# Attention and feed-forward sandwich: the last rows in a new order, the very last by column halves, x loaded by halves, w_o by one part a block

## The chip, the cores and the metric

The kernel runs on one core of one Trainium2 chip. The metric is the device time of one execution in microseconds (us), as a median over several runs. The engines of the core go by the profile's short names: PE (TensorE, matmuls and transposes through a matmul), PEld (its weight loads, which overlap PE), DVE (VectorE), ACT (ScalarE), POOL (GpSimd) and SP (SyncE, which here only issues DMAs).

## What is computed

One transformer layer over x, 1024 rows of 512 columns, all in fp32. The reference, shortened:

```python
x = x + layernorm(attention(layernorm(x), w_q, w_k, w_v, w_o))
x = x + layernorm(ffn(x, base_W, base_b, router_W, router_b, A, B, expert_map))

def attention(h, w_q, w_k, w_v, w_o):      # 32 query heads, 8 key/value heads of 128
    q, k, v = h @ w_q, h @ w_k, h @ w_v    # 4 query heads share one k, v
    scores = where(causal, q @ k.T / sqrt(128), -inf)
    return softmax(scores) @ v @ w_o

def ffn(x, ...):
    base_out = x @ base_W.T + base_b
    p = softmax(x @ router_W.T + router_b)       # 15 logits
    w = per-expert sums over expert_map of the 8 largest p   # 8 experts
    lora = ((x @ A.T) * w) @ B * 2               # rank 16 for each expert
    return base_out + lora
```

## The kernel before

**Tiling.** The 1024 rows are NT = 8 row tiles of 128. A key/value head with its R = 4 query heads is a group; there are G = 8. A block (g, t) is one group and one row tile; the list `blocks` has N = 64 of them, group by group. The first six groups take the row tiles in order. The last two (from block N2 on) go together by pairs of row tiles, in the order 0, 3, 2, 1, so that the row tiles of the last eight blocks can be finished one after the other. The last four rows to finish are c, d, e and f, row tiles 4, 5, 2 and 3, which belong to blocks N-6, N-5, N-2 and N-1.

**One block.** A block's scores are made in four sub-blocks (32 rows of each of the four heads): scores `s` on PE, the causal mask (L618) and the negated maximum `nmax` (L620) on DVE, the exponentials `p` with their sum on ACT (L625), the reciprocal `rec` (L631) on DVE, the product with it on ACT (L632), and a transpose within 32 x 32 squares into `T` (L638) on DVE. Where a sub-block doesn't reach the end of its row tile, POOL clears the rest of `p` (a memset, L623). Sixteen small DMAs, nearly all on SP, then bring `T` to the tile `K` with keys on partitions (`K<-T`). Two blocks later PE multiplies by `v` into `po`, ACT copies that to `attnT` (L669), and the output projection follows: for two row tiles at once in `project_o_pair`, which needs four sums and differences of `attnT` (L720 to L723, on DVE: sums, sums, attnT, sums) and has the products `pa` to `pe`, each added into `acc` by DVE (L744), for the last group by itself in `project_o` (`pO`). Projections of later blocks fill in on PE. Products of halves save matmuls: combined weights and inputs are made on POOL (`tx` by L188; `sq` and others by `combine_q`, L145; `combine_o`, L706).

**Order.** Every engine carries out its instructions in order. In the main loop the order comes from the loop itself and from a scheduler that sorts the instructions of each engine, save those given to `keep`, which stay in the order of the code. `loads(i)` issues the weight loads of later blocks at the head of block i, on SP. Loads of w_o: `load_o(g)` issues R = 4 parts of 256 KB (128 partitions of 512 fp32); it is called for g + 1 in the row t = 5 of the groups 0 to 5.

**Start.** x comes in by eight row-tile loads, alternately on SP and on ACT's queue, with the first weights between them. After a layer norm each row tile is transposed by PE (`ptx_x`); PE fills the time before with 26 transposes of the identity, `idle`.

**Last rows.** After the loop the order on all engines is written out: `run(pieces)` emits the pieces of PE work with what belongs to them; `go(rows)` emits the next deferred piece of a row's DVE, ACT and POOL work (`held`), and `work_off` emits deferred pieces within the scores. The pieces of a row after its attention: `ffn_norms` (statistics L288, normalising L300, adding x L777), `ffn_router` (transposes `ptx_h`; `pl`, the router's logits with the experts' first products; `route`, L813 to L830, softmax and the eight largest, which ends in `hw`), and `ffn_out` (`base`, the four pairs of `pf`; `turn_hw`, transpose `ptw` and copy `hwT`, L857; `finish`, the last pair of `pf` with `bt_sb`, the addition of the bias to `y`, L864, and the layer norm). For rows c, d, e that norm's scaling is on ACT (L303, L304) and its addition to `acc` on POOL (L870); for row f both are on DVE (L300, L870). The power -1/2 of every norm (`rstd`, L294) is on POOL. `ffn_store` stores a finished row. L103, L106 and L109 are the helpers of all matmuls, transposes and DMAs.

PSUM banks: `bank` gives the next of a ring of single banks in turn, so a product can start when the one that had that bank is read out; `ps_s` is the pool of the scores, whose tiles serve some `pf` as well.

Of the kernel before, what the change touches and what calls it, by code (L numbers as in the profile page):

```python
# [22 lines left out]
def kernel(  # L23
# [175 lines left out]
        for c in range(KC // 2):  # L199
            weights["v", gv, i * (KC // 2) + c] = w[:, c, :]  # L200

    def load_o(g, by=nc.scalar):
        wo = wp.tile([P, R, H], F32, tag="wo", name=f"wo_{g}")
        for j in range(R):
            load(wo[:, j, :], w_o[ts(g * R + j, P), :], by)
        weights["o", g] = wo

    def load_base(tag, cs, by=nc.scalar):
        for c in cs:
# [4 lines left out]
    x_in = turn_tile("K", "x", NT - 1).rearrange("p (t h) -> p t h", t=NT)  # L214
    two = (nc.sync, nc.scalar)

    def load_x(t):
        load(x_in[:, t, :], x[ts(t, P), :], two[t % 2])

    for t in range(2):  # L220
        load_x(t)
    for i in range(2):
        load_v(0, i, two[i])
    for t in range(2, TPB):
        load_x(t)
    load_k(0, nc.sync)
    for i in range(2):
        load_q(0, i, two[1 - i])
    for t in range(TPB, NT):
        load_x(t)  # L230

    ident = const.tile([P, P], F32, tag="ident", name="ident")
    make_identity(nc, ident)
    neg_half = const.tile([P, 1], F32, tag="neg_half", name="neg_half")
    nc.gpsimd.memset(neg_half, -0.5)

    xnT = [big.tile([P, KC, QB], F32, tag=f"xnT{b}", name=f"xnT_{b}") for b in range(NQB)]

# [362 lines left out]
    def scores(g, t, j):  # L601

        n = t * P + (j + 1) * SQ
        full = (t + 1) * P
        name = f"{g}_{t}_{j}"
        s = ps_s.tile([P, S], F32, tag="s", name=f"s_{name}")
        for c0 in range(0, n, QB):
            w = min(QB, n - c0)
            matmul(
                s[:, c0 : c0 + w],  # L610
                qTs[g, t // 2][:, (t % 2) * NSUB + j, :, :].rearrange("p h q -> p (h q)"),
                kTs[g, c0 // QB][:, :w],
                start=True,
                stop=True,
            )
        pin = keep if blocks.index((g, t)) >= N2 + 2 else lambda ins: ins
        rescale_scores()
        keep(nc.vector.tensor_tensor(s[:, n - SQ : n], s[:, n - SQ : n], smask, ALU.add))  # L618
        nmax = small.tile([P, 1], F32, tag="nmax", name=f"nmax_{name}")
        keep(nc.vector.tensor_reduce(nmax, s[:, :n], AX.X, ALU.max, negate=True))  # L620
        p = act.tile([P, S], F32, tag="p", name=f"p_{name}", bufs=3)
        if n < full:
            nc.gpsimd.memset(p[:, n:full], 0.0)  # L623
        total = small.tile([P, 1], F32, tag="total", name=f"total_{name}")
        keep(nc.scalar.activation(p[:, :n], s[:, :n], AF.Exp, bias=nmax, accum_out=total))  # L625
        finish_scores()
        work_off(1 + len(deferred) // 5)

        def rescale():
            rec = small.tile([P, 1], F32, tag="rec", name=f"rec_{name}")  # L630
            keep(nc.vector.reciprocal(rec, total))  # L631
            keep(nc.scalar.mul(p[:, :n], p[:, :n], rec))  # L632

        def finish():
            if j == 0:
                turned[g, t] = turn_view(turn_tile("T", g, t), t)
            pin(
                nc.vector.transpose(  # L638
                    turned[g, t][:, :, j, :, :].rearrange("p b k q -> p k b q"),
                    p[:, :full].rearrange("p (k b q) -> p k b q", b=R, q=SQ),  # L640
                )
            )
            if j == NSUB - 1:
                three = (nc.sync, nc.sync, nc.gpsimd)

                at = blocks.index((g, t))
                short = at < 1 or at < N2 and g % 2 and t in (1, 2, 3)
                alone = not short and at < N - 1
                to_keys(g, t, by=three[:1] if alone else three)

        score_tile["rescale"], score_tile["finish"] = rescale, finish
# [59 lines left out]
    def project_o_pair(g, u):  # L711

        hk = R // 2
        wo, wt = weights["o", g], weights["ot", g]
        a1 = attnT.pop((g, 2 * u)).rearrange("p (h q) -> p h q", q=P)
        a2 = attnT.pop((g, 2 * u + 1)).rearrange("p (h q) -> p h q", q=P)
        a11, a12, a21, a22 = a1[:, :hk], a1[:, hk:], a2[:, :hk], a2[:, hk:]
        sums = act.tile([P, 3, hk, P], F32, tag="sums", name=f"sums_{g}_{u}", bufs=1)
        s1, s2, s4 = (sums[:, n] for n in range(3))
        nc.vector.tensor_tensor(s1, a21, a22, ALU.add)  # L720
        nc.vector.tensor_tensor(s2, s1, a11, ALU.subtract)
        nc.vector.tensor_tensor(a21, a11, a21, ALU.subtract)
        nc.vector.tensor_tensor(s4, a12, s2, ALU.subtract)  # L723
        b11, t12, b21, b22 = wo[:, :hk, :hn], wo[:, :hk, hn:], wo[:, hk:, :hn], wo[:, hk:, hn:]
        to = sums_o[u]
        pm = {}

        def product(name, half, lhs, rhs, dst=None):


            def piece(k):
                if half == 0 and k == 0:
                    pm[name] = bank(f"p{name}_{g}_{u}").rearrange("p (a n) -> p a n", n=hn)
                matmul(
                    pm[name][:, half, :], lhs[:, k, :], rhs[:, k, :], start=(k == 0), stop=(k == hk - 1)
                )
                if k == hk - 1 and dst is not None:
                    src = pm[name][:, : half + 1, :]
                    if half == 0:
                        src = src.to_broadcast([P, dst.shape[1], hn])  # L740
                    if g == 0 and name in "ab":
                        nc.vector.tensor_copy(dst, src)
                    else:
                        nc.vector.tensor_tensor(dst, src, dst, ALU.add)  # L744

            return [(hn, lambda k=k: piece(k)) for k in range(hk)]

        def last():
            if g == G - 2:
                every = to[:, 0:1, :].to_broadcast([P, 4, hn])  # L750
                nc.vector.tensor_tensor(to[:, 1:, :], to[:, 1:, :], every, ALU.add)

        return (
            product("a", 0, a11, b11)
            + product("a", 1, a12, b21, to[:, 0:2, :])
            + product("b", 0, s2, wt[:, 1], to[:, 2:5, :])
            + product("c", 0, a21, wt[:, 0], to[:, 3:5, :])
            + product("d", 0, s1, t12, to[:, 2:5:2, :])
            + product("e", 0, s4, b22)
            + product("e", 1, a22, wt[:, 2], to[:, 2:4, :])  # L760
            + [(1, last)]
        )
# [77 lines left out]
    def ffn_out(t):  # L840
# [3 lines left out]
        def base(k):  # L844
            if k == 0:

                if t in (c, e, f):
                    pf.append(ps_s.tile([P, S], F32, tag="s", name=f"pf_{t}")[:, :512])
                else:
                    pf.append(bank(f"pf_{t}"))  # L850
            matmul(pf[0], state["hT", t][:, k, :], weights["base", k], start=(k == 0), stop=False)
# [9 lines left out]
        def finish():  # L861
            matmul(pf[0], state.pop(("hwT", t)), bt_sb, start=False, stop=True)
            y = ffn.tile([P, H], F32, tag="hy", name=f"y_{t}", bufs=3)
            order(nc.vector.tensor_tensor(y, pf[0], bias_bc, ALU.add))  # L864
            by = nc.vector if t == f else nc.gpsimd
            statistics, norm = layernorm(y, y, f"y{t}", nc.vector if t == f else nc.scalar)

            def add_y():
                norm()
                order(by.tensor_tensor(acc[t], y, acc[t], ALU.add))  # L870
                state["done", t] = True

            defer(t, statistics, add_y)

        w = [(512, lambda k=k: base(k)) for k in range(KC)]
        return w[:2], [(P, turn_hw)], w[2:], [(512, finish)]

    def ffn_store(t):
        assert state["done", t]
# [41 lines left out]
    def loads(i):  # L921
# [7 lines left out]
        if i < N2:  # L929
# [10 lines left out]
            if t == 6 and (g + 1) % GV == 0:  # L940
                for j in range(2):
                    load_v((g + 1) // GV, j, by)
            if t == 5:
                load_o(g + 1, by)
        elif i == N2 + 3:
            load_o(G - 1, by)
        elif i == N2 + 4:
            load_base("wk", (0, 1), by)
        elif i == N2 + 7:
            load_base("wv", (2, 3), by)  # L950
# [44 lines left out]
    run(first_q[: 2 * KC] + project_k(0, 0) + first_q[2 * KC :])  # L995
    for t in range(TPB, TPB + 2):
        input_turn(t)
    load_o(0, nc.sync)

    def complete(i, *behind):  # L1000

# [73 lines left out]
        ffn_store(t)  # L1075
    (turn_d, products_d), (turn_e, products_e), (turn_f, products_f) = map(ffn_router, (d, e, f))
    out_c, out_d, out_e, out_f = map(ffn_out, (c, d, e, f))
    run(o_pair[:8] + out_c[0] + out_c[2] + o_pair[8:16] + [turn_d] + o_pair[16:])
    run(attend(N - 2) + [products_d])
    go(d)  # L1080
    run(out_c[1] + project_o(*blocks[N - 2]))
    go(e)
    run(out_c[3])
    go(e, e)
    run(attend(N - 1) + project_o(*blocks[N - 1]))
    go(e, f, c, f, f)
    run(out_d[0] + out_d[1] + out_d[2] + [turn_e] + out_d[3])
    go(f, c)
# [1 line left out]
    go(d, e)  # L1090
    run(out_e[0] + out_e[2][:1] + [turn_f] + out_e[2][1:] + [products_f])
    go(d, f)
    run(out_f[0] + out_e[1] + out_f[2][:1] + out_e[3])
    go(e)
    run(out_f[2][1:] + out_f[1])
    go(e)
    run(out_f[3])
    go(f, f)
    for t in (c, d, e, f):
        ffn_store(t)  # L1100

# [40 lines left out]
```

## Time and profile before

| what | us |
|---|---|
| median of 3 runs | 1066.59 (1066.48 to 1067.16) |
| the profiled execution's own time | 1066.64 |
| its span, first to last instruction | 1064.9 |
| PE busy in the span | 1046.5 |
| end of the last matmul, from the span's start | 1055.74 |

The profiled execution is 0.05 us from the median. All times inside a trace are counted from the span's start; the execution's own time is 1.74 us more than the span. The granted TensorE clock was 0.996 of full speed. The costliest groups of the page's part 5 give the durations that recur below: after the line, the engine and the operation come the tiles written and read with their shapes, the count, then the busy time and the mean of one in ns, then the engine's idle time just before these instructions and what ended most of it:

```profile
L103 PE MATMUL po<-K,v 128*128 128x512 f32 x576 | 280.3, 594 | 1.7 <-DMA wo<-in_w_o_dram 1.0
L103 PE MATMUL s<-kT,qT 128*128 128x512 f32 (+15 forms) x768 | 272.4, 463 | 1.4 <-ACT p L625 1.3
L638 DVE STREAM_TRANSPOSE T<-p 128x128 f32<-128x128 f32 (+7 forms) x256 | 197.7, 774 | 52.5 <-ACT p L632 37.9
L188 POOL TENSOR_TENSOR tx<-xnT 128x256 f32<-128x256 f32 x52 | 37.9, 729 | 209.8 <-PE pv L103 124.6
```

A matmul's duration counts its pipeline too, so neighbours overlap: eight in a row of `pO` take 3.44 us and not eight times 0.6. What PE waited for, the ends of the critical stretches and the instructions that the change moves are shown in the prediction.

### The profile page before, as it was taken

The page shows a single profiled execution, that of the slowest core. Times are in us where ns is not written, and L with a number is a line of the kernel's source. Part 1 is how long each engine was busy: PE and PEld are TensorE (multiplying, and loading weights), DVE is VectorE, ACT ScalarE, POOL GpSimd, SP SyncE. Part 2 cuts the span into 40 slices and gives each one's busy share as a digit, 9 for nine tenths or more (in the row PEclk, how much of TensorE's full clock was granted, in tenths as well). Part 3 has the DMA queues.
Part 4 walks back from the last instruction along what each step waited for, and adds up shares of the span by engine and source line. Part 5 has one row for each costly group of instructions (what it writes and reads, how often), then busy time and mean ns, then how long its engine had stood idle before and what let it go on. Part 6 is the DMA issues. An engine that isn't in the chain of part 4 may idle for free.

```text
span 1064.9 us, 15423 instructions
## 1 busy us (share of the span) xinstructions
PE 1046.5 (98%) x4782; PEld 729.8 (69%) x4782; DVE 740.1 (70%) x1810; ACT 480.7 (45%) x965; POOL 255.0 (24%) x491
## 2 busy tenths in 40 slices
PE   9999999999999999999999999999999999999996
PEld 7766667767777676767777667767787566466553
DVE  4586657876687766877577776887457766576756
ACT  3655435553344534553245544554235554353421
POOL 2613125241131215241130313351130110111212
PEclk9999999999999999999999999999999999999998
DMA  5146352563125442463225352464523754444231
GB/s 188 34 115 149 70 121 70 150 154 86 27 56 154 104 108 72 115 158 79 61 50 131 102 125 61 127 160 109 129 66 104 183 143 111 125 110 106 69 84 40
DMA packets 78513, 111.99 MB, mean 105 GB/s; under 512 B 18176, under 2 KB 49920, under 8 KB 78432
## 3 DMA queue, kind: packets, MB, share of 16 engines
q1 hardware_dynamic: 74960, 105.71, 39.5%
q0 software_dynamic: 2096, 3.46, 1.4%
q10 hardware_dynamic: 1376, 1.84, 0.5%
q8 instruction: 39, 0.64, 0.3%
q14 instruction: 42, 0.34, 0.1%
HBM read 33.34 MB, written 2.10 MB: 33 GB/s over the span
## 4 chain that ended last, share of the span: by engine, by line
PE 90%; DVE 3%; SPq 3%; ACT 1%; DMA 1%; issue 1%; POOL 0%; POOLq 0%; DVEq 0%; ACTq 0%
PE po L103 22%; PE s L103 20%; PE pq L103 19%; PE pv L103 5%; PE pe L103 4%; PE pa L103 4%; PE pk L103 4%; PE pf L103 3%; PE pO L103 3%; SPq L109 3%; PE pc L103 2%; PE pb L103 2%; PE pd L103 2%; PE pl L103 1%; DMA wo<-in_w_o_dram 1%
## 5 line engine op out<-in xcount | busy, mean ns | idle before, releaser
L632 ACT ACTIVATE p<-p,rec 128x32 f32<-128x32 f32 (+31 forms) x256 | 188.3, 736 | 225.8 <-DVE rec L631 164.8
L103 PE MATMUL po<-K,v 128*128 128x512 f32 x576 | 280.3, 594 | 1.7 <-DMA wo<-in_w_o_dram 1.0
L103 PE MATMUL s<-kT,qT 128*128 128x512 f32 (+15 forms) x768 | 272.4, 463 | 1.4 <-ACT p L625 1.3
L625 ACT ACTIVATE p<-s,nmax 128x32 f32<-128x32 f32 (+31 forms) x256 | 179.5, 701 | 163.1 <-DVE nmax L620 147.2
L638 DVE STREAM_TRANSPOSE T<-p 128x128 f32<-128x128 f32 (+7 forms) x256 | 197.7, 774 | 52.5 <-ACT p L632 37.9
L103 PEld LDWEIGHTS s<-kT,qT 128*128 128x128 f32 x768 | 141.2, 190 | 118.2 <-issue 105.9
L620 DVE TENSOR_REDUCE nmax<-s 128x1 f32<-128x32 f32 (+31 forms) x256 | 180.2, 704 | 7.3
L103 PEld LDWEIGHTS po<-K,v 128*128 128x128 f32 x576 | 103.6, 190 | 61.7 <-issue 51.4
L623 POOL MEMSET p<- 128x96 f32 (+2 forms) x192 | 29.3, 157 | 423.2 <-DVE T L638 377.5
L618 DVE TENSOR_TENSOR s<-s,smask 128x32 f32<-128x32 f32 x256 | 48.0, 187 | 99.4 <-PE s L103 98.8
L103 PE MATMUL pq<-xnT,wq 128*128 128x128 f32 (+1 forms) x656 | 113.3, 321 | 0.0
L103 PEld LDWEIGHTS pq<-xnT,wq 128*128 128x128 f32 x656 | 99.5, 191 | 14.0 <-issue 7.2
L188 POOL TENSOR_TENSOR tx<-xnT 128x256 f32<-128x256 f32 x52 | 37.9, 729 | 209.8 <-PE pv L103 124.6
L450 DVE TENSOR_TENSOR qT<-pq,qT 128x256 f32<-128x256 f32 x138 | 62.0, 460 | 32.0 <-ACT qT L476 18.9
L669 ACT COPY attnT<-po 128x512 f32<-128x512 f32 x64 | 37.4, 584 | 76.5 <-PE po L103 76.3
L103 PE MATMUL pa<-wo,attnT 128*128 128x256 f32 x224 | 58.8, 385 | 0.0
L103 PEld LDWEIGHTS pq<-tx,wq 128*128 128x128 f32 x368 | 47.1, 192 | 7.6 <-issue 7.5
L103 PEld LDWEIGHTS pq<-tx,sq 128*128 128x128 f32 x368 | 47.5, 192 | 5.7 <-issue 5.0
L103 PE MATMUL pq<-tx,sq 128*128 128x128 f32 x368 | 51.2, 275 | 0.0
L103 PEld LDWEIGHTS pa<-wo,attnT 128*128 128x128 f32 x224 | 41.0, 190 | 14.0 <-issue 9.3
L625 ACT ACTIVATION_READ_ACCUMULATOR p<-s,nmax 128x1 f32 x256 | 49.5, 193 | 0.0
L103 PE MATMUL pq<-tx,wq 128*128 128x128 f32 x368 | 49.2, 275 | 0.0
(146 smaller groups left out, 1258.4 us busy)
## 6 DMA issues: line engine op xcount, KB each, us to landing
K<-T SPq DMA_DIRECT2D x128, 128.0 KB, 2.4
K<-T SPq DMA_DIRECT2D x128, 112.0 KB, 2.3
wq<-in_w_q_dram SPq DMA_DIRECT2D x27, 512.0 KB, 4.8
K<-T SPq DMA_DIRECT2D x128, 96.0 KB, 2.2
K<-T SPq DMA_DIRECT2D x128, 80.0 KB, 2.1
wo<-in_w_o_dram SPq DMA_DIRECT2D x32, 256.0 KB, 3.9
K<-T SPq DMA_DIRECT2D x108, 64.0 KB, 2.0
K<-T SPq DMA_DIRECT2D x113, 48.0 KB, 2.0
```

What stands on the lines that cost most here:

```text
L103: keep(nc.tensor.matmul(*args, **kw))
L109: keep(by.dma_start(dst, src))
L188: nc.gpsimd.tensor_tensor(dst, p, q, ALU.subtract)
L450: nc.vector.tensor_tensor(dst, src, to, ALU.add)
L618: keep(nc.vector.tensor_tensor(s[:, n - SQ : n], s[:, n - SQ : n], smask, ALU.add))
L620: keep(nc.vector.tensor_reduce(nmax, s[:, :n], AX.X, ALU.max, negate=True))
L623: nc.gpsimd.memset(p[:, n:full], 0.0)
L625: keep(nc.scalar.activation(p[:, :n], s[:, :n], AF.Exp, bias=nmax, accum_out=total))
L632: keep(nc.scalar.mul(p[:, :n], p[:, :n], rec))
L638: nc.vector.transpose(turned[g, t][:, :, j, :, :].rearrange("p b k q -> p k b q"), p[:, :full].rearrange("p (k b q) -> p k b q", b=R, q=SQ),)
L669: copy = nc.scalar.copy(o, po)
```

## The change

- **Start.** Row tiles 0 and 1 of x are loaded in two halves of 64 partitions each, one on SP, one on ACT's queue. Row tiles 4 to 7 all go to SP. ACT makes a copy of one column (`warm`) ahead of its other work.
- **w_o.** `load_o` takes the parts that it is to load: for groups 1 to 6 one part in each of the rows t = 4, 5, 6, 7. Group 0 and group 7 are loaded at once as before.
- **Last rows.** `work_off` is left out of the very last sub-block of scores. The four sums of the last pair are pinned in their place on DVE. Row c's four `pf` pairs follow `pa` (after four pieces instead of eight), row d's transposes follow the next six. `attend(N - 1)`, the `po` of the last block, stands ahead of the `finish` of row c.
- **Row f.** `ffn_out_last` makes `pf` in two halves of 256 columns in two banks. The bias and the statistics go by halves as well, all on DVE; then the mean is subtracted by a tensor_scalar, and a scalar_tensor_tensor multiplies by `rstd` and adds `acc` in one instruction, where a norm (tensor_scalar with mean and `rstd`) and an addition were. All of it is pinned.

In the scheduled order of instructions, PE and DVE have the same order as before between the start and the last rows. SP differs by the places of the w_o parts. POOL differs in the blocks (2, 6) and (4, 6), where `combine_q` stands ahead of a memset of `p` that it followed before.

```diff
-    def load_o(g, by=nc.scalar):
-        wo = wp.tile([P, R, H], F32, tag="wo", name=f"wo_{g}")
-        for j in range(R):
-            load(wo[:, j, :], w_o[ts(g * R + j, P), :], by)
-        weights["o", g] = wo
+    def load_o(g, rows, by=nc.sync):
+        if 0 in rows:
+            weights["o", g] = wp.tile([P, R, H], F32, tag="wo", name=f"wo_{g}")
+        for j in rows:
+            load(weights["o", g][:, j, :], w_o[ts(g * R + j, P), :], by)
...
     for t in range(2):
-        load_x(t)
+        for n in range(2):
+            half = slice(n * (P // 2), (n + 1) * (P // 2))
+            load(x_in[half, t, :], x[ts(2 * t + n, P // 2), :], two[n])
     for i in range(2):
         load_v(0, i, two[i])
     for t in range(2, TPB):
-        load_x(t)
+        load_x(t, two[t % 2])
     load_k(0, nc.sync)
     for i in range(2):
         load_q(0, i, two[1 - i])
     for t in range(TPB, NT):
-        load_x(t)
+        load_x(t, nc.sync)
...
+    keep(nc.scalar.copy(const.tile([P, 1], F32, tag="warm", name="warm"), neg_half))
...
-        work_off(1 + len(deferred) // 5)
+        if (g, t, j) != (*blocks[-1], NSUB - 1):
+            work_off(1 + len(deferred) // 5)
...
+        pin = keep if (g, u) == pairs[-2] else lambda ins: ins
...
-        nc.vector.tensor_tensor(s1, a21, a22, ALU.add)
+        pin(nc.vector.tensor_tensor(s1, a21, a22, ALU.add))
...
+    def ffn_out_last(t):
+        halves = [slice(n * hn, (n + 1) * hn) for n in range(2)]
+        pf = {}
+        def base(n, k):
+            if k == 0 and n == 0:
+                pf[n] = ps_s.tile([P, S], F32, tag="s", name=f"pf_{t}_{n}")[:, :hn]
+            elif k == 0:
+                pf[n] = bank(f"pf_{t}_{n}")[:, :hn]
+            w = weights["base", k][:, halves[n]]
+            matmul(pf[n], state["hT", t][:, k, :], w, start=(k == 0), stop=False)
+        def finish():
...
+            for n in range(2):
+                matmul(pf[n], hwT, bt_sb[:, halves[n]], start=False, stop=True)
+                keep(nc.vector.tensor_tensor(y[:, halves[n]], pf[n], bias_bc[:, halves[n]], ALU.add))
+                keep(nc.vector.bn_stats(stats[:, n, :], y[:, halves[n]]))
+            keep(nc.vector.bn_aggr(mv, stats))
+            keep(nc.vector.tensor_scalar(ve, mv[:, 1:2], EPS, None, ALU.add))
+            keep(nc.gpsimd.tensor_tensor(rstd, ve, neg_half, ALU.pow))
+            keep(nc.vector.tensor_scalar(y, y, mv[:, 0:1], None, ALU.subtract))
+            keep(nc.vector.scalar_tensor_tensor(acc[t], y, rstd, acc[t], ALU.mult, ALU.add))
...
-            if t == 5:
-                load_o(g + 1, by)
+            if t >= NT - R:
+                load_o(g + 1, (t - NT + R,))
...
-    run(o_pair[:8] + out_c[0] + out_c[2] + o_pair[8:16] + [turn_d] + o_pair[16:])
+    run(o_pair[:4] + out_c[0] + out_c[2] + o_pair[4:10] + [turn_d] + o_pair[10:])
     run(attend(N - 2) + [products_d])
     go(d)
     run(out_c[1] + project_o(*blocks[N - 2]))
     go(e)
-    run(out_c[3])
+    run(attend(N - 1) + out_c[3])
     go(e, e)
-    run(attend(N - 1) + project_o(*blocks[N - 1]))
+    run(project_o(*blocks[N - 1]))
...
-    run(out_f[0] + out_e[1] + out_f[2][:1] + out_e[3])
+    (first, second), finish_f = ffn_out_last(f)
+    run(first + out_e[1] + second[:2] + out_e[3])
     go(e)
-    run(out_f[2][1:] + out_f[1])
+    run(second[2:] + out_f[1])
     go(e)
-    run(out_f[3])
-    go(f, f)
+    finish_f()
```

## The prediction, made before the changed kernel ran

> **What bounds the kernel now.** I read the page's busy shares first, then what TensorE (PE) waited for, then the timeline of the stretches that the change touches. The page:
>
> ```profile
> span 1064.9 us, 15423 instructions
> PE 1046.5 (98%) x4782; PEld 729.8 (69%) x4782; DVE 740.1 (70%) x1810; ACT 480.7 (45%) x965; POOL 255.0 (24%) x491
> ```
>
> PE has work in all but 18.4 us, and the chain of waits gives PE 90% of the span. The diff adds no PE work: the last row's 512-wide matmuls become twice as many of half the width (a 256-wide pair takes 0.43 us in the pb row, a 512-wide one 0.86). So only the 18.4 us can be won. The waits of PE say which are stalls:
>
> ```profile
> PE idle L106 <- POOL ident masks.py:199: 1.5, 1, 1.5
> PE s L103 <- ACT p L625: 1.3, 4, 0.3
> PE pb L103 <- DVE top L817: 1.1, 1, 1.1
> PE po L103 <- DMA wo<-in_w_o_dram: 1.0, 2, 0.5
> PE pO L103 <- ACT attnT L669: 0.7, 1, 0.7
> PE pc L103 <- DVE acc L744: 0.5, 1, 0.5
> PE pf L103 <- ACT hwT L857: 0.4, 1, 0.4
> PE ptx_x L106 <- DVE K_x L341: 0.4, 1, 0.4
> ```
>
> Columns: total, times, longest. The rest of the 18.4 is the end: the last matmul stops at 1055.74 and 9.2 us of VectorE (DVE), GpSimd (POOL), the store (1060.35 to 1062.35) and the program's end follow. The pb and pc stalls are one place, in the last rows:
>
> ```profile
> 1012.88 0.40 DVE L720 TENSOR_TENSOR sums<-attnT 128x256 f32<-128x256 f32 x1
> 1013.34 0.42 DVE L721 TENSOR_TENSOR sums<-sums,attnT 128x256 f32<-128x256 f32 x1
> 1013.90 1.10 PE L103 MATMUL pb<-wot,sums 128*128 128x256 f32 x4 [1.10 <-DVE top L817]
> 1015.48 1.10 PE L103 MATMUL pc<-wot,attnT 128*128 128x256 f32 x4 [0.47 <-DVE acc L744]
> ```
>
> pa ended at 1012.80; pb needs the second sum; the routing of row c, between the sums on DVE, makes it late. The end:
>
> ```profile
> 1056.04 0.21 DVE L303 TENSOR_SCALAR shift_y<-mv_y,rstd_y 128x1 f32<-128x1 f32 x1 [0.73 <-POOL rstd_y L294]
> 1056.17 0.68 DVE L864 TENSOR_TENSOR y<-pf,bias_bc 128x512 f32<-128x512 f32 x1
> 1057.24 1.26 POOL L870 TENSOR_TENSOR acc<-y,acc 128x512 f32<-128x512 f32 x1 [1.23 <-ACT y L304]
> 1058.46 0.55 POOL L294 TENSOR_TENSOR rstd_y<-ve_y,neg_half 128x1 f32<-128x1 f32 x1
> 1059.05 0.55 DVE L300 TENSOR_SCALAR y<-y,mv_y,rstd_y 128x512 f32<-128x512 f32 x1 [1.06 <-POOL rstd_y L294]
> ```
>
> Row f's y starts 0.43 us after the matmul's end: DVE sits on row e's shift (L303). Its rstd then stands behind row e's add on POOL.
>
> **What the Trainium skill says.** "SBUF — State Buffer", section "Who interferes with whom": DVE and GpSimd share a port pair, an exclusive lock held for a whole instruction; a DVE operation with two SBUF inputs contends with a GpSimd one that reads SBUF, tensor_scalar can too, and whoever issues first blocks the other. The trace agrees: sums at 311.18 took 0.86 us instead of 0.43 and ended about when POOL's tx (311.04 to 311.77) did; sel at 1051.53 took 1.10 while POOL's add (1051.33 to 1052.60) ran. "VectorE: DVE Perf Modes", section "The TRN2 errata", gives (N+151)/0.96 ns for an fp32 tensor_tensor: 0.42 for 256 and 0.69 for 512, as sums and the last add measure. "DMA: Bandwidth & Descriptors", section "Issuing engines are not separate DMA queues": a second issuing engine saves issue time alone. Here an issue took about 0.4 us on SP (0.74 to 1.13), against 3.7 us to landing.
>
> **The change part by part**, in the profiled execution's clock.
>
> *Last rows, reordered.* pf of row c (four pairs, 3.43 us) goes between pa and pb: 1012.80 to 1016.23. The sums are now pinned ahead of the routing on DVE; with the reciprocal, one accumulation (0.69) and the sums (0.42 each, starts 0.34 to 0.47 apart) the second ends near 1014.8 and the fourth near 1015.4. So pb's 1.10 goes, and pc's 0.47. pb and pc then run 1016.23 to 1017.95. The routing of c now comes later: its last product hw frees the bank that pd takes, near 1018.1, and the accumulations of pb and pc free those of the transposes and of pe; I put 0.3 to 0.5 for these new waits in all (DVE: 0.69 and 0.95 for acc, 1.5 for the routing chain, from 1016.1). Then pd 0.86, transposes 0.44, pe 1.73 end at about 1022.0, po of block N-2 (2.57) at 1024.6, pl 0.98 with ptw 0.11 at 1025.7, pO (3.44) at 1029.1. Block N-1's po (3.45) now comes before row c's bt pair (0.86): 1032.6, then 1033.4. The copy of po to attnT (0.59, in ACT) lies beneath that pair, so pO's wait of 0.68 goes and it ends at 1036.9, where it ended at 1038.81. Gain 1.10 + 0.47 + 0.68 less the new waits 0.3: **1.94**, bounds 1.5 to 2.2. Queued behind the last block's T are 16 key DMAs, eleven on SP (0.63 us each) and five on POOL: with T at 1015.4 to 1016.1 they start near 1016.1 instead of 1019.14, so the last lands near 1024.4 instead of 1027.37; po of N-1 needs it at 1029.1. The loads of x for rows e and f (1026.08), behind them on SP, come earlier too. After pO PE runs into pl of row f as before, and DVE (normalising h of rows e and f) moves along with it; so all arrives 1.94 earlier.
>
> *Last row by halves.* y of the first half could start one bt half earlier, but DVE is held by row e's statistics and shift (1056.04), not by PE. Two half adds and two half statistics cost about 0.2 more than 0.68 + 0.69 (the fixed part twice, by the formula 0.16 each, partly overlapped). That lies beneath POOL's add for row e (to 1058.50), which holds rstd as before. What is won comes after: before, norm (0.55) and add (0.69) follow rstd (1059.01) and end at 1060.32. Now y minus mean needs no rstd, and one scalar_tensor_tensor follows. The trace shows no such operation; it has the two SBUF inputs of a 512-wide add, so I take 0.69. The subtraction wants the shared port, which POOL's add holds until 1058.50; then it competes with rstd (0.55 alone, 0.72 to 0.78 where they overlap elsewhere in this trace). End near 1059.97: gain **0.35**. Below: nothing, if the subtraction and rstd run one after the other; above: 0.55, the whole norm.
>
> *First rows of x.* x0 lands at 4.45; 26 filler transposes occupy PE to 6.70 and the first real one starts at 7.08, a wait of 0.38. The halves make x0 land earlier by less than the 0.4 of an issue; wk waits for the first half (the order of instructions against before shows it), wq0 for the second, and x4 goes to SP. At best 0.38 less, since the fillers cover the rest; at worst wq0, landed 10.30 before and needed at 13.79, or x2 (7.70) come late, for which 3.5 and 2.5 us are spare. I take **0.3**, 0 for the low end. The early small ScalarE copy pulls the table load (6.42 to 7.70) out of that wait's neighbourhood; counted in the 0.3.
>
> *w_o by one part a block.* Four loads of 256 KB at t=5 become one each at t=4 to 7 in groups 0 to 5. The two po waits of 0.55 are put down to these loads. But the last key DMA landed at 327.93 and 573.62, 3.6 us after issue instead of the usual 2.0, just before po began (328.27, 573.86). In both places a 16 KB instruction fetch of PE runs, which delays key DMAs elsewhere with no w_o near (one issued at 203.36 landed at 207.09), while w_o right behind key DMAs at 193.34 left them at 2.02. The fetch recurs with the same PE stream. So **0**, at best 1.1. Each load stands in an SP gap (308.12 to 314.88 between two blocks' key DMAs, against 0.4 of issue); the tightest key landing has 0.20 us of slack (block 7), so below it I allow 0.3.
>
> *combine_q on POOL.* In two blocks (group 2 and 4, t=6) the order comparison puts its four 1.27 us additions ahead of a memset that waited for DVE:
>
> ```profile
> 349.42 0.12 POOL L623 MEMSET p<- 128x32 f32 x1 [3.93 <-DVE T L638]
> 349.50 1.28 POOL L145 TENSOR_TENSOR sq<-wq 128x512 f32<-128x512 f32 x1
> 345.69 0.43 DVE L720 TENSOR_TENSOR sums<-attnT 128x256 f32<-128x256 f32 x1 [1.29 <-ACT attnT L669]
> ```
>
> They now start at about 345.5 and meet the four sums (345.69 to 347.25), all with two SBUF inputs. If DVE slips in after the first addition, the sums are late by 1.1, if it waits for two, by 2.15, if for all, by 4.75. Queued behind them are reciprocal, nmax, T, and for these PE: scores at 352.78 need the exponentials of 349.5, so 3.2 us are spare there; pb at 350.20 needs the second sum (346.57), 3.6. I take 0, hidden in these; at worst 1.8 a block.
>
> Sum: 1.94 + 0.35 + 0.3 = **2.6 us** off the profiled execution's 1066.64 (span 1064.9 plus 1.74), which is 0.05 from the median 1066.59: **1064.0 us**.
>
> **The rivals.** *Port starvation* (the other side): POOL's four additions keep the lock back to back; past 3.2 us of delay, PE stalls by 1.5 to 1.8 in both blocks, 3.6 in all: 1064.0 + 3.6 = 1067.6, slower than before. If a head loss joins in, 1068.8. For it: 0.86 instead of 0.43 at 311.18; against: there DVE got in after one tx, though more followed. *The end is fixed*: the subtraction and rstd exclude each other, the head wait stays, new waits of pd and pe cost 0.8: 1.5 gained, 1065.1, within 0.2%. For it: rstd lengthens beside tensor_scalar. Against: the pinned order leaves DVE time. *w_o was the cause*: both po waits go too, 1.1 more: 1062.9. For it, the releaser named; against, the fetches. *The change doesn't do what it says in the tail*: another wait (pd on hw, the last keys) takes all that pb gave back, 0.6 left, 1066.0.
>
> **How the numbers follow.** Chances: forecast 0.52, w_o 0.12, end fixed 0.18, tail lost 0.08, port starvation 0.10. 0.2% (2.1 us) is about what a measurement can tell from no change, so faster means below 1064.46. The forecast's own bounds (1063.3 to 1064.8) fall below that for about nine tenths; with w_o that is 0.60. Starvation exceeds +2.1 in about half of its cases: slower 0.05. The rest, 0.35, is within. The range 1062.6 to 1066.0 holds all but starvation, the worst of tail loss and luck beyond w_o. The likeliest case's own range is 1063.3 to 1064.8.
>
> **What would show it.** Right: pb and pc without waits, pO of N-1 directly after pf, ending some 1.9 before 1038.81; y subtracted before rstd; the first ptx_x near 6.7. Wrong: pd waiting over 0.5; sums near 345.7 ending after 350; a new wait on wq or K<-T; the two po waits gone. A last scalar_tensor_tensor well above 0.69 would eat the halves' gain.

## The result, and the profile after

| | before | after |
|---|---|---|
| median, us (7 runs each, side by side) | 1066.52 (1065.73 to 1067.16) | 1069.81 (1067.85 to 1070.88) |
| ratio, 95% interval | | 1.0027 (1.0017 to 1.0037) |
| profiled execution, us | 1066.64 | 1068.83 |
| its span, us | 1064.9 | 1067.1 |

By the ratio the change made the kernel slower by about 2.9 us (1.8 to 3.9; the two medians lie 3.3 apart); 2.6 us less had been predicted. The runs of the changed kernel spread over 3 us, and the profiled one, at 1068.83, lies in their lower half: what its trace accounts for is its own 2.2 us. The page and the waits of PE (total, times, longest):

```profile
PE 1047.8 (98%) x4792; PEld 732.1 (69%) x4792; DVE 748.0 (70%) x1812; ACT 480.4 (45%) x966; POOL 255.5 (24%) x491
```

```profile
PE s L103 <- ACT p L629: 2.7, 6, 0.7
PE po L103 <- DMA K<-T: 1.0, 2, 0.7
PE ptx_x L106 <- DVE K_x L345: 0.9, 2, 0.8
PE po L103 <- ACT p L629: 0.9, 1, 0.9
PE pd L103 <- DVE hw L836: 0.3, 1, 0.3
PE pf L103 <- ACT hwT L863: 0.4, 1, 0.4
```

The waits of pb, pc and pO in the last rows (1.1, 0.5 and 0.7 before) are gone, as foreseen; pd has a small one. But the scores wait 2.7 instead of 1.3, po has a new wait of 0.9 on ACT's exponentials, and the first transposes wait 0.9 instead of 0.4. (What po waits on keys, 1.0, is not new in sum: before it was 0.5, with 1.0 more that the view put to w_o.) To see where, I set the two traces side by side, one PE instruction against the same one, and note where the distance jumps:

| from the start of | in before | jump, us | distance after it |
|---|---|---|---|
| first ptx_x, pv | 7.08 to 11.5 | +0.84 | 0.84 |
| po at three key waits | 150.78, 328.27, 573.86 | -0.26, -0.14, -0.56 | |
| block (2, 6): scores, then po | 352.78, 363.57 | +0.83, +1.17 | 2.45 |
| block (4, 6): scores, then po | 598.37, 609.16 | +0.82, +1.01 | 3.71 |
| po | 702.74 | +0.17 | 3.89 |
| last rows, up to the last bt pair | 1013.90 to 1052.22 | -1.97 | 1.92 |
| last addition of row f | 1060.32 (its end) | -0.35 | 1.57 |
| end of the span | 1064.87 | +0.6 | 2.2 |

Two blocks cost 3.8 us, all that the last rows won and more. Their timeline in the changed kernel, first DVE, then POOL (start, duration):

```profile
346.14 1.31 DVE L726 TENSOR_TENSOR sums<-attnT 128x256 f32<-128x256 f32 x1 [1.30 <-ACT attnT L674]
347.49 1.37 DVE L727 TENSOR_TENSOR sums<-sums,attnT 128x256 f32<-128x256 f32 x1
348.78 1.48 DVE L728 TENSOR_TENSOR attnT<-attnT,attnT 128x256 f32<-128x256 f32 x1
350.19 1.49 DVE L729 TENSOR_TENSOR sums<-attnT,sums 128x256 f32<-128x256 f32 x1
351.60 0.15 DVE L636 RECIPROCAL rec<-total 128x1 f32<-128x1 f32 x1
```

```profile
345.90 1.27 POOL L145 TENSOR_TENSOR sq<-wq 128x512 f32<-128x512 f32 x1
347.25 1.33 POOL L145 TENSOR_TENSOR sq<-sq,wq 128x512 f32<-128x512 f32 x1
348.54 1.44 POOL L145 TENSOR_TENSOR wq<-wq,wq 128x512 f32<-128x512 f32 x1
349.94 1.45 POOL L145 TENSOR_TENSOR sq<-wq,sq 128x512 f32<-128x512 f32 x1
```

Read them together: each sum on DVE ends 0.3 us after the POOL addition that started before it, and the next POOL addition starts 0.2 to 0.3 before the sum's end. The two engines take turns, instruction by instruction, and four sums of 0.43 us become four of 1.3 to 1.5. The reciprocal comes at 351.60 instead of 347.17, 4.4 us late; the trace was 0.45 behind already, so the meeting itself costs DVE 4.0. That delay reaches PE twice:

```profile
354.06 1.72 PE L103 MATMUL s<-kT,qT 128*128 128x512 f32 x4 [0.67 <-ACT p L629]
...
366.02 1.10 PE L103 MATMUL po<-K,v 128*128 128x512 f32 x2 [0.90 <-ACT p L629]
```

First the scores, which need the exponentials two sub-blocks earlier; 3.2 us of spare time absorbed the rest. Then po of block (2, 5): its keys start on SP when the delayed T is done (353.85 instead of 349.43) and sixteen DMAs follow one another; the last landed at 365.53 instead of 361.08, and po had been at 363.57. The name that the view puts to that second wait (ACT p) misleads; the landing of the keys, 0.5 us before po begins, is what came last. The same four sums and four additions meet at 593.16 in block (4, 6), with the same durations to 0.01 us.

### The profile page after: what moved, and what is told of

It reads as the page before. It is cut to its first block, busy times and chain, and to the rows that moved or that the text cites. A ratio compares the mean times of both kernels' runs of the same rounds, so it can differ in the third digit from the quotient of the medians.

```text
span 1067.1 us, 15452 instructions
## 1 busy us (share of the span) xinstructions
PE 1047.8 (98%) x4792; PEld 732.1 (69%) x4792; DVE 748.0 (70%) x1812; ACT 480.4 (45%) x966; POOL 255.5 (24%) x491
## 3 DMA queue, kind: packets, MB, share of 16 engines
q10 hardware_dynamic: 1104, 1.31, 0.4%
## 4 chain that ended last, share of the span: by engine, by line
PE 88%; DVE 5%; SPq 2%; ACT 1%; DMA 1%; issue 1%; POOL 0%; POOLq 0%; DVEq 0%; ACTq 0%
PE po L103 22%; PE s L103 19%; PE pq L103 18%; PE pk L103 5%; PE pv L103 4%; PE pe L103 4%; PE pa L103 4%; PE pO L103 3%; PE pf L103 2%; PE pc L103 2%; SPq L109 2%; PE pb L103 2%; PE pd L103 2%; DVE T L643 1%; DVE nmax L624 1%
## 5 line engine op out<-in xcount | busy, mean ns | idle before, releaser
L636 DVE RECIPROCAL rec<-total 128x1 f32<-128x1 f32 x256 | 39.2, 153 | 15.3 <-ACT p L629 13.9
```

## The experiments

Each time stands beside runs of the kernel before on the same chip; I compare by the ratio to these.

**e1.** The swap on POOL undone, nothing else.

```diff
+            clear = nc.gpsimd.memset(p[:, n:full], 0.0)
+            if (g, t, j) in ((2, 6, 2), (4, 6, 2)):
+                keep(clear)
...
-                if n == 1:
+                if n == (2 if blocks[i] in ((2, 6), (4, 6)) else 1):
                     combine_q(m)
```

> The changed kernel, with nothing altered but two places of one POOL instruction: in blocks (2, 6) and (4, 6) the memset of p stands ahead of combine_q again, as in the kernel before, so that the four additions of combine_q start only after the four sums on DVE. The w_o parts stay spread. Theory A (port lock): the sums go back to 0.43 us each, the T of those blocks is 4.4 us earlier, the waits of scores (0.83) and of po (1.2 and 1.0) there vanish; about 3.8 us less than the changed kernel, near 1066.0. Theory B (the w_o parts on SP hold up the keys of those blocks): no change from the changed kernel, near 1069.8.

Measured: 1064.73 us, ratio 0.9987 (0.9980 to 0.9993); against the changed kernel's 1.0027 that is 0.40%, 4.3 us. The sums in its timeline, and POOL beside them:

```profile
346.27 0.42 DVE L728 TENSOR_TENSOR sums<-attnT 128x256 f32<-128x256 f32 x1 [1.30 <-ACT attnT L676]
346.73 0.42 DVE L729 TENSOR_TENSOR sums<-sums,attnT 128x256 f32<-128x256 f32 x1
...
349.99 0.12 POOL L627 MEMSET p<- 128x32 f32 x1 [3.92 <-DVE T L645]
350.07 1.27 POOL L145 TENSOR_TENSOR sq<-wq 128x512 f32<-128x512 f32 x1
```

The memset waits 3.92 us for DVE and holds combine_q back until the sums are over. The w_o parts lay on SP exactly as in the changed kernel, so they are not the cause.

**e5.** The converse: the kernel before with the memset pinned behind combine_q (the first three lines of e1's edit alone).

> The kernel before, with nothing altered but two places of one POOL instruction: in blocks (2, 6) and (4, 6) the memset of p is pinned behind combine_q, as the changed kernel has it. w_o loads, start and last rows as before. Theory A (the port lock alone costs what the changed kernel lost there): the sums take 1.3 to 1.5 us each, scores and po wait in both blocks, 3.8 us more than before, near 1070.1. Theory B (it takes the spread w_o parts too): less than 1 us more, under 1067.3.

Measured: 1070.06 us, ratio 1.0038 (1.0025 to 1.0050). In its trace these two memsets are all that stands elsewhere than before, on any engine, and the turns are there again:

```profile
345.13 1.27 POOL L145 TENSOR_TENSOR sq<-wq 128x512 f32<-128x512 f32 x1
345.38 1.31 DVE L722 TENSOR_TENSOR sums<-attnT 128x256 f32<-128x256 f32 x1 [1.30 <-ACT attnT L671]
```

PE's jumps against before are 0.83 and 1.09 in block (2, 6), 0.82 and 1.11 in (4, 6), about 3.85 in all. The loss of the two blocks is shown from both sides.

**e6.** The kernel before with w_o by one part a block alone (the edit of `load_o` and `loads` in the diff).

> The kernel before with w_o by one part a block alone, which brings the swap on POOL with it. Theory A: the swap costs 3.8 and the spreading itself nothing or a gain of up to 1: 1069.1 to 1070.1, within 1 us of e5. Theory B (spreading itself costs on SP): above e5.

Measured: 1069.41 us, ratio 1.0035 (1.0023 to 1.0048), the same as e5 within the intervals. The scheduler moves the memset behind combine_q as soon as the w_o loads are spread, with nothing else changed. So it is this part of the change that brought the collision, through an order on an engine that it doesn't name.

**e3.** The kernel before with the changed last rows alone.

> The kernel before with the changed last rows alone (order of the rows, row f by halves): start and w_o loads as before. Theory A (the tail gains as the hand sum has it, 1.94 + 0.35): 2.3 us less than before, near 1064.2. Theory B (the new waits for hw and the ending eat most of it): 0 to 1 us less, 1065.5 to 1066.5.

Measured: 1064.09 us, ratio 0.9981 (0.9973 to 0.9989), 2.0 us less. Run again beside e13 and e14 as e15:

> e3 again, beside e13 and e14: near 1064.1, the span ending 5.2 after the last addition.

Measured: 1064.30 us, ratio 0.9980 (0.9973 to 0.9987). The tail is a gain. Parts measured alone add up: e6 (+3.7), e7 below (+1.4) and e3 (-2.0) make +3.1, against +2.9 for the whole change.

**e7.** The kernel before with the changed start alone.

> The kernel before with the changed start alone (rows 0 and 1 of x by halves on two queues, rows 4 to 7 on SP, the early copy on ACT). Theory A (each half costs more issue time than a whole row, so row 1, wv and rows 2 and 3 land about 1 us late): 0.8 to 1.6 us more than before, first pq near 14.7 to 15.4 instead of 13.79 us. Theory B (the start's loss is made up by waits further on): within 0.3 us of before.

Measured: 1066.94 us, ratio 1.0013 (1.0006 to 1.0019), 1.4 us more. SP's queue and PE in its timeline:

```profile
0.74 1.47 SPq L109 DMA_DIRECT2D K_x<-in_x_dram  x2
2.25 0.60 SPq L109 DMA_DIRECT2D wv<-in_w_v_dram  x1
2.89 0.47 SPq L109 DMA_DIRECT2D K_x<-in_x_dram  x1
...
7.38 0.66 PE L106 MATMUL ptx_x<-ident,K_x 128*128 128x128 f32 x4 [1.36 <-DVE K_x L345]
...
11.88 0.66 PE L106 MATMUL ptx_x<-ident,K_x 128*128 128x128 f32 x4 [0.75 <-DVE K_x L345]
```

SP in the kernel before:

```profile
0.74 0.39 SPq L109 DMA_DIRECT2D K_x<-in_x_dram  x1
1.19 0.42 SPq L109 DMA_DIRECT2D wv<-in_w_v_dram  x1
1.65 0.47 SPq L109 DMA_DIRECT2D K_x<-in_x_dram  x1
```

Issuing the two halves takes 1.47 us on SP, where the kernel before issued one whole row in 0.39 and half of wv from 1.19 on. Now that part of wv goes out at 2.25 and lands 1.7 us later than before; row 2 goes out at 2.89 and lands 1.1 later. First row 0 is late: on DVE its normalising stands behind row 1's statistics, and row 1 lands at 5.67 here and at 6.22 in the changed kernel (4.68 before), though row 0 itself lands at 3.84 (4.45 before).

The issue times don't account for all of it. Four traces have this start unaltered (the changed kernel, e1, e7 and e8). In all of them ACT's half of row 1 goes out at 1.33 or 1.34, but it lands between 4.43 and 6.64, and the first pq begins between 14.54 and 15.99; the ten traces with whole rows have 13.79 to 13.99. So one start loses 0.75 to 2.2 us from trace to trace, and the 0.84 of the profiled run is near the low end. Why the landings scatter stays open.

**e2.** The changed kernel with row 0 normalised before row 1's statistics.

```diff
             begin(t)
-            if n:
+            if t == 0:
+                end(t)
+            elif n and rows[n - 1]:
                 end(rows[n - 1])
```

> The changed kernel, but on DVE row 0 of x is normalised before the statistics of row 1 instead of after them. Theory A (the late landing of row 1's halves holds up row 0's normalising through DVE's order): the first ptx_x starts when the fillers end, about 7.2 instead of 7.92 us, 0.7 us less, near 1069.1. Theory B (the start is bound by row 1 to 3 and the weights behind the halved loads): the wait only moves to the next ptx_x or pv, and the time stays near 1069.8.

Measured: 1069.56 us, ratio 1.0032 (1.0021 to 1.0044): no gain.

```profile
6.64 0.66 PE L106 MATMUL ptx_x<-ident,K_x 128*128 128x128 f32 x4 [0.51 <-DVE K_x L345]
8.16 1.97 PE L103 MATMUL pv<-wv,xnT 128*128 128x256 f32 x8 [0.43 <-DMA wv<-in_w_v_dram]
10.88 0.63 PE L106 MATMUL ptx_x<-ident,K_x 128*128 128x128 f32 x4 [0.75 <-PE pv L103]
12.29 0.66 PE L106 MATMUL ptx_x<-ident,K_x 128*128 128x128 f32 x4 [0.79 <-DVE K_x L345]
```

The first transposes come 1.28 earlier than in the changed kernel, and then pv waits for wv and the third for row 2: the second theory holds. DVE's order was only the first of several waits on loads that all go out late. **e4** puts e1 and e2 together:

> e1 and e2 together. If the port lock and the order of row 0 and row 1 are the two losses and add up, 3.8 + 0.7 less than the changed kernel: near 1065.3, faster than before by about 1.2. If either only exposes another wait, 1066 or more.

Measured: 1064.74 us, ratio 0.9988 (0.9980 to 0.9996), the same as e1 alone; the second half of the expectation missed, as in e2.

**e9.** e3 with, of the start, only row 0 by halves; row 1 whole on ACT.

> The kernel before with the changed last rows and, of the start, only row 0 of x by halves on two queues; row 1 whole on ACT, rows 4 to 7 alternating, no early copy. Compared with e3. Theory A (issue time of the halves delays what is behind them on both queues): SP issues one half in place of one whole and wv there goes out at most 0.2 later, on ACT one DMA more goes ahead; row 1 lands near 5.4, the loss against e3 is under half of that of the whole changed start, 0.2 to 0.5 us. Theory B (halves land late by themselves, whatever is issued behind): row 0 lands later than 4.5.

Measured: 1065.54 us, ratio 0.9996 (0.9988 to 1.0004), against 0.9981 for e3. Row 0 landed at 4.11 and row 1 at 5.16, so row 0's halves were not late by themselves; but the loss (0.9 us in the trace once the scores run, 1.6 by the ratios) was well above what I had put, and its place another one: pv began at 9.67 instead of 8.51, behind the copy of the first transposes. On ACT the order was:

```profile
5.18 2.52 ACTq L109 DMA_DIRECT2D K_x<-in_x_dram  x2
7.74 1.28 ACT L324 ACT_TABLE_LOAD   x1 [7.74 <-DMA wv<-in_w_v_dram]
9.03 0.58 ACT L324 COPY xnT<-ptx_x 128x512 f32<-128x512 f32 x1
```

The table load stands behind two loads of x that wait for earlier ones. In the changed kernel the early copy and the move of rows 4 to 7 to SP put the table load at 4.24 (6.42 before, with whole rows): that edit does its work, but in part against a delay that the halves made.

**e8.** The changed kernel with row f as before.

> The changed kernel with row f finished as before: one bank, 512 columns, norm and addition after rstd. Theory A (halves gain 0.35 at the end): from shift of row e to the end of the last addition 4.28 instead of 3.93 us, 0.35 more than the changed kernel, near 1070.1. Theory B (the halves give nothing or cost): the same or less than the changed kernel.

Measured: 1068.71 us, ratio 1.0028 (1.0017 to 1.0040), the same as the changed kernel by time. In the traces the last addition ends 4.27 after the start of row e's shift, and 3.93 in the changed kernel: 0.34 won, as expected. But from there to the end of the span it takes 4.55 (1062.58 to 1067.1), and 5.2 in the changed kernel (1061.88 to 1067.1). e13 and e14 take that apart. **e13** is e3 with row f as before; **e14** is e13 with the mean subtracted early and the scalar_tensor_tensor, but one bank of 512 columns:

```diff
-            statistics, norm = layernorm(y, y, f"y{t}", nc.vector if t == f else nc.scalar)
...
+                    keep(nc.vector.tensor_scalar(y, y, mv[:, 0:1], None, ALU.subtract))
+                    keep(nc.vector.scalar_tensor_tensor(acc[t], y, rstd, acc[t], ALU.mult, ALU.add))
```

> The kernel before with the reordered last rows, row f as before (one bank, norm and addition after rstd). Theory A (the column halves bring the late end): last addition 0.35 later than in e3 against the end of PE, but the span ends 4.55 after it instead of 5.2: 0.3 us less than e3, near 1063.8. Theory B (the late end comes with the reordering): 0.35 more than e3, near 1064.4.

Measured: 1063.92 us, ratio 0.9976 (0.9967 to 0.9986).

> e13, but for row f the mean is subtracted ahead of rstd and one scalar_tensor_tensor ends the row, still in one bank of 512 columns. Theory A (the early subtraction alone wins the 0.35, the column halves win nothing since POOL's add of row e covers them): from shift of row e to the end of the last instruction 3.9 instead of 4.28 us. Where the span then ends 4.55 after it, the late end belongs to the column halves; where 5.2, to the new last instructions.

Measured: 1064.21 us, ratio 0.9980 (0.9973 to 0.9986). The end of row f in e14, then in e15 (with halves):

```profile
1054.15 0.21 DVE L304 TENSOR_SCALAR shift_y<-mv_y,rstd_y 128x1 f32<-128x1 f32 x1 [0.73 <-POOL rstd_y L295]
...
1056.01 0.88 DVE L890 TENSOR_SCALAR y<-y,mv_y 128x512 f32<-128x512 f32 x1
1056.57 0.73 POOL L887 TENSOR_TENSOR rstd_y<-ve_y,neg_half 128x1 f32<-128x1 f32 x1
1057.34 0.75 DVE L891 SCALAR_TENSOR_TENSOR acc<-y,rstd_y,acc 128x512 f32<-128x512 f32 x1 [0.44 <-POOL rstd_y L887]
```

```profile
1053.66 0.21 DVE L304 TENSOR_SCALAR shift_y<-mv_y,rstd_y 128x1 f32<-128x1 f32 x1 [0.73 <-POOL rstd_y L295]
...
1055.80 0.61 DVE L909 TENSOR_SCALAR y<-y,mv_y 128x512 f32<-128x512 f32 x1
1056.08 0.73 POOL L907 TENSOR_TENSOR rstd_y<-ve_y,neg_half 128x1 f32<-128x1 f32 x1
1056.85 0.75 DVE L910 SCALAR_TENSOR_TENSOR acc<-y,rstd_y,acc 128x512 f32<-128x512 f32 x1 [0.44 <-POOL rstd_y L907]
```

From shift to the end of the last addition both take 3.94, and e13 4.27: the column halves win nothing, since POOL's addition for row e covers them, and the early subtraction wins the 0.34 by itself. After it the span ends 5.1 later in both, 4.55 in e13. So the late end comes with the new last instructions and not with the halves. The traces say through what: POOL. Its last instruction is row f's rstd, which takes 0.73 beside the subtraction and 0.55 in e13. Behind it in POOL's order stand only the instructions of the program's end, first a drain, which waits and is not counted as busy; its record begins even before that of rstd. In e13 (of the three drains: shortest, median and longest in ns, then the first and the last start in us; the first is the longest):

```profile
1055.86 0.55 POOL L295 TENSOR_TENSOR rstd_y<-ve_y,neg_half 128x1 f32<-128x1 f32 x1
L1176 POOLq DRAIN  x3: 46/102/5971, 1055.5 to 1062.0; - x3
```

and in e14:

```profile
L1197 POOLq DRAIN  x3: 46/102/6157, 1056.2 to 1062.9; - x3
```

That first drain ends 5.07 or 5.08 us after the end of rstd in all 17 traces of this case, and the span 0.8 to 0.9 after the drain. Counted from the last addition, the drain ends about 3.76 later where a norm and an addition end the row and 4.28 later where scalar_tensor_tensor does; the last store has landed about 1.7 us before that in the one case, 2.25 in the other. So the span's end hangs on POOL's last instruction: the 0.34 won behind rstd is off the path, and the 0.18 by which rstd grew is lost. This is read from the traces; no run moved POOL's last instruction by itself. By time e13, e14 and e15 can't be told apart.

**e10, e11, e12.** Three attempts at a faster kernel: e10 is e3 with the first norms in another order on DVE (row 0 at once; statistics of rows 1 and 2; both normalised; row 3), e11 the changed kernel with the start of before and e1's edit, e12 both.

> e3 (last rows alone) with the layer norms of the first rows in another order on DVE: row 0 is normalised at once, then statistics of rows 1 and 2, then both normalised, then row 3. Hoped for as the fastest: the first ptx_x at 6.9 instead of 7.1 and the third near 10.4 instead of 10.8; 0.2 to 0.5 us less than e3, near 1063.8. If the fillers or wv set that stretch, no change.

Measured: 1064.84 us, ratio 0.9987 (0.9980 to 0.9993). The first ptx_x stayed at 7.19, since the statistics of row 0 began only at 4.58 and the rest follows: no gain.

> The changed kernel with the start of before and the memset ahead of combine_q: last rows and spread w_o parts kept. If spreading w_o is worth nothing by itself, as I predicted, it is equal to e3 within 0.3 us, near 1064.1; if the two po waits were caused by w_o, 0.5 to 1 less, near 1063.3.

Measured: 1064.27 us, ratio 0.9981 (0.9975 to 0.9988), as e3: spreading w_o is worth nothing that could be measured once its side effect is gone.

> e11 with the order of the first norms of e10: by the same amount faster than e11 as e10 than e3, 0.2 to 0.5.

Measured: 1064.51 us, ratio 0.9984 (0.9978 to 0.9991): as e11, so the expected gain is missing here too. The lowest ratio of all is that of e13, the reordered rows and nothing else, 2.5 us below before; its interval overlaps those of e3, e11, e14 and e15.

## Why the prediction was wrong

- **combine_q on POOL, cost put at 0: wrong, and the step that decided.** I saw the swap, the meeting with the four sums and the lock, and even listed 4.75 as the worst delay of DVE. The trace has 4.0 from the meeting: POOL and DVE take turns, so every sum waits for a whole addition of 1.27. I had reckoned that the delay, whichever it was, would be hidden; DVE did slip in after one addition, the mildest of my cases, but after one sum the next addition was ahead of it again. (My delays for two and for four additions, 2.15 and 4.75, come out as about 2.35 and 4.9 from my own 345.5 and 1.27.) The cover failed too: I checked the delay against the scores (3.2 us spare) and pb, but not against T, the keys and the po after next, whose keys had 2.5 us to spare. Measured 3.8 for both blocks. The port-starvation rival had 3.6, with a head loss 1068.8, but only the chance of 0.10, and my range left it out. It was right in kind, by turns instead of back to back; that the profiled time is 1068.83 is in part luck, since the rival had neither the key waits (-0.79) nor the late end (+0.6), which nearly cancel.
- **First rows of x, -0.3: wrong sign.** It measured +0.84 in the changed kernel's trace and +1.4 by time alone (e7). The step that failed is "the halves make x0 land earlier by less than the 0.4 of an issue": I priced an issue at 0.4 whatever its shape and counted it for row 0 only. The halves took 0.56 to 0.83 each, and what stands behind them on both queues went out about 1 us later. Row 0 did land 0.65 earlier, but its normalising waits on DVE behind row 1's statistics. The Trainium skill's "DMA: Bandwidth & Descriptors", section "Issuing engines are not separate DMA queues", calls the time to initiate a DMA usually small relative to the DMA itself. In the changed kernel the halves took 2.6 to 4.8 us from the start of the issue to landing, so 0.56 to 0.82 was small beside that, but not for what stood behind. The later issues go with a loss of about 1 us; the scatter of the landings, with which it reaches 2.2 in e8, is not explained.
- **Last rows reordered, -1.94: right in sum, with two terms mis-sized.** From the start of pa to row d's first pf PE took 27.73 us before and 25.83 after: 1.90 less. Counted from starts, with 0.86 for each group of four, the waits that went were 1.27 (pb), 0.72 (pc) and 0.85 (pO), 2.8 instead of my 2.25, since the ends that I had read are modelled ones; the new ones were 1.0 (pd 0.43, transposes 0.12, pe 0.36 and 0.11), of which I had put 0.3. The two errors made up for each other. My running clock has a slip that the 1.94 does not use: from pd at 1018.1 its own terms lead to 1021.4 to 1021.6, not 1022.0; and behind pO comes row d's pf, not row f's pl. pb itself runs without a wait:

```profile
1016.44 3.60 PE L103 MATMUL pf<-wbase,hT 128*128 128x512 f32 x8
1019.88 1.03 PE L103 MATMUL pb<-wot,sums 128*128 128x256 f32 x4
1020.74 1.03 PE L103 MATMUL pc<-wot,attnT 128*128 128x256 f32 x4
1022.03 1.13 PE L103 MATMUL pd<-wo,sums 128*128 128x256 f32 x4 [0.26 <-DVE hw L836]
```

- **Last row, -0.35: right up to the last addition, but that was not the path to the end.** scalar_tensor_tensor took 0.75 (I took 0.69), rstd 0.73 beside the subtraction. I had kept the stretch after the last addition at its length of before; it grew by about 0.6, because by the traces the span's end follows POOL's rstd, which ended 0.17 later after row e's shift. From that shift to the end of the span it took 8.83 before and 9.10 in the changed kernel (8.82 in e13, 9.01 in e14), so this part costs 0.2 to 0.3. Too little for the times to show.
- **w_o, 0: right by itself** (e11 against e3), but wrong as a part of the change, since it is what swaps POOL's order (e6). The prediction told of the swap under a heading of its own and never tied it to a part. The po waits that the view puts to w_o differ from kernel to kernel whatever the loads do: 0.2 in e3 and 1.4 in e14, neither with spread w_o, and 0.6 in e11, with it; in e7, with the loads as before, none is left. Nor does a late key need w_o: in the changed kernel one issued at 569.28 takes 3.77 us to land, and the next part of w_o goes out only at 574.20.

The sum by its own terms, in the profiled execution: +0.84 + 3.83 - 0.79 (key waits, net) - 1.97 - 0.35 + 0.6 = +2.2, which is its difference. I had -2.6 with the first at -0.3, the second at 0, no key waits and no late end.

## What to carry to other kernels

When a change moves SBUF-only work of one engine beside that of the other on the shared port, count turns, as in these traces: every instruction of DVE waited for a whole instruction of POOL, and the delay must be followed along all that hangs on the delayed engine, to the next consumer of its DMAs, not only to the first. Where a scheduler sets an order, look at the order on every engine after a change that touches just one, and pin what matters: here two memsets were worth 4 us. Cutting a first load in two pays only if what stands behind it on the queues can bear the second issue. And before the last row is shortened, see what ends the span: here it followed POOL's last instruction, not the last addition.

## What the runs showed of the hardware that I had not expected

- DVE and POOL, both with two SBUF inputs and work queued, alternated one instruction each in both blocks of the changed kernel and in e5: sums of 0.42 us took 1.31 to 1.49 beside additions of 1.27, which themselves lengthened to 1.45. The Trainium skill's "SBUF — State Buffer", section "Who interferes with whom", says that the shared port pair is an exclusive lock and that a DVE instruction with two SBUF inputs contends with a GpSimd one that reads SBUF. The traces agree; the taking of turns is what they add.
- As the first DMA of SP's or ACT's queue, a load of 64 partitions took 0.56 to 0.60 us to issue, one of 128 partitions with the same row length 0.38 to 0.42 (all 17 traces). The loads right behind a half were slow to issue too, whatever their shape: a second half 0.61 and 0.83, a whole row 0.59 and a part of wv 0.81 (both in e9). No run parts the shape from the place in the queue further.
- POOL's drain at the program's end was over 5.07 or 5.08 us after POOL's last instruction in all 17 traces, and the span ended 0.8 to 0.9 after it. The last store had landed 1.7 to 2.3 us before that drain was over, so in these kernels it was not the store that ended the span, as far as the traces tell.
